# The values of the second cross-attention, made in the experts' stage instead of in layer 1's self-attention, and a block attention that ends in another order

## The chip, the core and the metric

The kernel runs on one core of one Trainium2 chip. The core has a matrix engine (TensorE, PE in the profile; its weight loads are listed as PEld), a vector engine (DVE), a scalar engine (ACT), GpSimd (POOL) and a sync engine (SP), which issues most of the DMAs. Matmuls write to eight banks of PSUM, called `bank[0]` to `bank[7]` here. The metric is the device time of one execution in microseconds; lower is better. Before the change it is 2019.05 us, the median of three runs (2017.79 to 2019.08).

## The reference, cut to what matters

Two decoder layers work on x of 8 sequences with 112 tokens of 512 features, in float32. Layer 0 has a self-attention, a cross-attention on a context of 8 x 375 rows, and a "block": an attention with 32 heads of 128 and a mixture of 32 experts of which each token takes 8, beside a shared expert. Layer 1 has a self-attention, a second cross-attention on the same context, and a feed-forward part.

```python
x = x + _L0_attn_ref(_layernorm(x), ...)
x = x + _L0_xattn_ref(_layernorm(x), ctx_2048, ...)
x = x + _L0_ffn_ref(_layernorm(x), ...)          # block attention, then experts
x = x + _L1_attn_ref(_layernorm(x), ...)
x = x + _L1_xattn_ref(_layernorm(x), ctx_2048, ...)
x = x + _L1_ffn_ref(_layernorm(x), ...)

# in _L0_ffn_ref, after the block attention
h = _rmsnorm(x, ln2_w)
router_scores = jax.nn.sigmoid(t @ Wr)
_, idx = jax.lax.top_k(router_scores + expert_bias[None, :], TOPK)

# in _L1_xattn_ref
k = (memory_tokens @ wk.T).reshape(B, M, NH, HD)
v = (memory_tokens @ wv.T).reshape(B, M, NH, HD)
```

The keys and values `k` and `v` of the second cross-attention depend on the context and on weights only, so they can be made at any time before they are used. The mask of the context leaves only its last 96 rows (`TAIL`) to be attended to here, so a sequence's values are one product of 96 x 512 by 512 x 512.

## The kernel before

The 896 tokens are kept as 7 tiles `x[t]` of 128 tokens. Each stage norms the tiles, turns them into `hT` (features on the partitions), projects, attends sequence by sequence, and adds the result to x or y.

**Who sets the order.** A planner orders the instructions of each engine ahead of time: among those that it takes to be ready, the one that comes first in the program goes first, and a tile gets a buffer when one comes free. Engines run their lists strictly in that order. Inside `with in_order():` the order of the program is kept on ACT, DVE, POOL and PE (not on SP). Such instructions all carry line L80 in the profile, since a helper issues them, and the profile leaves out the digits of names: `c1_wv` is `c_wv` there, `a1_wo` is `a_wo`.

**Weights and rows.** `load_w` loads 1 MB of weights into one of the six buffers of `wp`. Buffers are handed on as their last readers finish, and SP waits in its queue at a load whose buffer is not free. `normed_rows()` gives one of three buffers `xn`, which hold normed tiles, copies of products, and rows on their way to DRAM.

**The end of the block attention** (`l0_block_attention`). Head groups `hg` 0 to 7 go over the sequences `b` 0 to 7. Beside scores, softmax and averages, PE is given pieces of larger products from two lists by `fill`: `output_products(oT, wo, columns, p)` adds tiles 2p and 2p+1 of the attention's output to y, `last_output` adds tile 6 by way of bank 2. `wanted` holds how many pieces of each list a head group is to take, and the number given with `add` says how many averages must be done first. In the last group `prepare()` loads the constants of the experts (`expert_constants`), and the output products of the group itself follow, for p = 1 and 2 and the last tile after the loop. `gather_weights` copies the experts' weights into one DRAM table on SP, in 64 steps.

**The experts' norm and sort** (`l0_block_experts`). The phase `e0` opens when the attention's memory is free. `rmsnorm_rows_T` squares each tile on ACT (into bank 2 or 3, L1238), scales it on DVE (L1241), stores it to `hrows` for later gathers, and turns it on PE (L235) into `hT`. The router's matmuls (`lg`, L259) follow, then the sigmoid and, in program order, the sort: DVE finds the eight experts of each token and counts places, while PE runs the matmuls of the shared expert (`fill`, with `wgus`) between small counting matmuls. `names_of(t, n)` makes one-hot matrices on DVE, scales one on ACT, and adds them up on PE; `shared_out(t)` is the second matmul of the shared expert. Then POOL gathers the rows and weights of the 66 or more blocks, and the experts run. `tp_ps()` hands out banks 4 and 5 in turn for transposes.

**Layer 1's self-attention** (`l1_self_attention`) goes over 16 steps n, two for each sequence, and four more to empty the pipeline. In each step DVE adds biases to scores, finds minima, and sums exponentials; ACT takes the exponentials; POOL divides; PE makes scores, turns probabilities and averages. In steps 0 to 7 it has a projection to make besides (`chunk`). In steps 8 to 15 it makes the values of the second cross-attention instead (`far`), one sequence a step:

```python
                    if n >= B and n < 2 * B:
                        cT = work[0].tile([P, KC, TAIL], FP, tag="cTv", name="cTv")
                        nc.sync.dma_start(cT, a["ctxT"][n - B][:, :, EARLY:])
                        far = last_values(n - B, cT, c1_wv)
                        step(far)
                        step(far)
```

`last_values` multiplies on PE into a bank of `tp_ps()`, copies the 96 x 512 result into an `xn` buffer on ACT, and stores it to `far_values` in DRAM, from where the second cross-attention loads it. Each matmul call in float32 shows as two instructions in the trace.

Of the kernel before, what the change touches and what calls it, by code (L numbers as in the profile page):

```python
# [30 lines left out]
P = 128  # L31
# [6 lines left out]
KC = D // P  # L38
# [20 lines left out]
def decoder(ctx: ExitStack, tc: tile.TileContext, a, out: bass.AP):  # L59
# [874 lines left out]
    def l0_block_attention(y, hT, late, weights, prepare):  # L934
# [11 lines left out]
        with phase("f0", "tile") as p0:  # L946
# [215 lines left out]
            for hg in range(8):  # L1162
                wo = load_w(a["f0_wo"][hg], "f0_wo")
                oT = p0.tile([P, 4, NT], FP, tag="oT", name="oT", bufs=2)
                if hg < 7:
                    qT_next, wq = new_queries(hg + 1)
                else:
                    prepare()
                done = hg * B
                given[:] = 0, 0  # L1170
                wanted[:] = 16 * (hg < 7), 25 if hg else 9
                if rest:
                    add(1, output_products(*rest, 1), done - 3)
                if hg < 7:
                    for p in range(2):
                        add(0, query_products(qT_next, wq, p))
                else:
                    wanted[:] = 16, 13
                if rest:
                    if hg < 7:  # L1180
                        add(1, output_products(*rest, 2), done - 1)
                    else:
                        add(0, output_products(*rest, 2, 0), done - 1)
                    add(1, last_output(*rest[:2]), done)
                for b in range(B):
                    if b == 3 and hg in (2, 4):

                        kv = hg // 2 + 1
                        keys[kv % 2], values[kv % 2] = new_keys(), new_values()
                        nc.sync.dma_start(keys[kv % 2], far_k[kv - 2])  # L1190
                        nc.sync.dma_start(values[kv % 2], far_v[:, :, (kv - 2) * P : (kv - 1) * P])
                    scores(hg, qT, b)
                    fill((3 * b + 1) / (3 * B))
                    s, mn = find_minima()
                    waiting.append((hg, oT, b, s))
                    if undivided:
                        divide(*undivided.pop())
                    one = waiting.pop(0) if len(waiting) > 2 else None
                    if one:
                        pT = turned(one[3])  # L1200
                    fill((3 * b + 2) / (3 * B))
                    if one:
                        average(*one[:3], pT)
                        averaged[0] += 1
                        make_ready()
                    if b == 4:
                        columns = output_sums(wo)
                    if b == 5:
                        add(int(hg < 7), output_products(oT, wo, columns, 0, int(hg < 7)), done + 3)
                    undivided.append(exps(s, mn))  # L1210
                    gather_weights(hg * B + b, undivided[0][1])
                    fill((3 * b + 3) / (3 * B))
                while later:
                    rope_halves(*later.pop(0))
                qT, rest = qT_next, (oT, wo, columns)
            divide(*undivided.pop())
            for one in waiting:
# [2 lines left out]
                average(*one[:3], turned(one[3]))  # L1220
                averaged[0] += 1
                make_ready()
            add(1, output_products(*rest, 1))
            add(0, output_products(*rest, 2, 0))
            add(1, last_output(*rest[:2]))
            while lists[0] or lists[1]:
# [5 lines left out]
    def rmsnorm_rows_T(hT, rows, src, weight):  # L1232


        for t in range(NTT):
            sq = sc_ps()
            c = sm.tile([P, 2], FP, tag="rms", name="rms", bufs=8)
            A.activation(sq, src[t], AF.Square, scale=D**-0.5, accum_out=c[:, 0:1])  # L1238
            rsqrt(c[:, 1:2], c[:, 0:1], ONCE)
            xn = normed_rows()  # L1240
            V.tensor_scalar_mul(xn, src[t], c[:, 1:2])  # L1241
            nc.sync.dma_start(rows[t * P : (t + 1) * P, :D], xn)
            transpose_tile(hT, xn, t, weight)

    def expert_constants(pool, accs):

        wr = pool.tile([P, KC, NEXP], FP, tag="wr", name="wr")
        nc.sync.dma_start(wr, a["e0_wr"])
        ebias = pool.tile([P, NEXP], FP, tag="ebias", name="ebias")
        nc.sync.dma_start(ebias, a["e0_bias"].partition_broadcast(P))  # L1250
        wgus = wp.tile([P, 2, KC, NI], FP, tag="w", name="wgus")
        wds = wp.tile([P, 2, D], FP, tag="w", name="wds")
        nc.sync.dma_start(wgus[:, 0], a["e0_wsg"])
        nc.sync.dma_start(wgus[:, 1], a["e0_wsu"])
        nc.sync.dma_start(wds, a["e0_wsd"])
        zero = normed_rows()
        G.memset(zero, 0.0)
        for acc in accs:
            nc.sync.dma_start(acc[NT:, :], zero)
        return wr, ebias, wgus, wds  # L1260

    def l0_block_experts(yp, y, weights, accs, constants):

# [7 lines left out]
        with phase("e0") as p0:  # L1271
# [1 line left out]
            sort = ExitStack()  # L1273
            sp = sort.enter_context(tc.tile_pool(name="sort", bufs=1))
            hrows = tc.dram_tile([NT, D + NEXP], FP, name="hrows")
            wr, ebias, wgus, wds = constants


            def counted(name, rows, n, base, step, mult, dtype=FP, pool=None):
# [28 lines left out]
            for t in range(NTT):  # L1308
                V.tensor_scalar(token[:, t : t + 1], part, 128.0, 2.0**t, ALU.add, ALU.mult)
            hT = new_hT()  # L1310
            rmsnorm_rows_T(hT, hrows, y, ln2w)
            for t in range(NTT):
                G.tensor_tensor(y[t], y[t], x[t], ALU.add)
                nc.sync.dma_start(accs[0][t * P : (t + 1) * P, :], y[t])
# [62 lines left out]
            with in_order():  # L1377
# [123 lines left out]
                        T.matmul(names[:, :SLOTS], atlow[:, k, :], athigh[:, k, :],  # L1501
                                 start=(t == 0 and k == 0), stop=(t == NTT - 1 and k == TOPK - 1))

                shared_banks = bank[4:6] + bank[7:] + bank[2:4] + bank[:2]

                def shared_out(t):

# [8 lines left out]

                fill(4)
                product()
                names_of(0, 2)
                names_of(1, 3)  # L1520
                names_of(2, 3)
                product()
# [1 line left out]
                product()  # L1524
                token_weights()
                for t in range(4, NTT):
                    shared_out(t - 4)
                    names_of(t, 0)

                name = sp.tile([P, SLOTS], FP, tag="name", name="name")  # L1530
                V.tensor_copy(name, names[:, :SLOTS])
# [125 lines left out]
    def l1_self_attention():  # L1657
# [2 lines left out]

        wq, wk_, wv, wo, c1_wv = (
            load_w(a[n], n) for n in ("a1_wq", "a1_wk", "a1_wv", "a1_wo", "c1_wv")
        )
        with phase("a1", "tile") as p0:


# [190 lines left out]

            next_hT = [None]  # L1860
            with in_order():
                chunk = out = vals = far = None
                norms = [next_rows(t) for t in range(NTT)]
                take_scores(0)
                mask_queries(1)
                for n in range(STEPS + 4):


                    b, odd = divmod(n - 4, 2)
                    sums = average(b) if 0 <= b < B and not odd else None  # L1870
                    if n < STEPS:
                        add_biases(n)
                        if not odd:
                            vals = values(n // 2)
                        step(vals)
                    elif n == STEPS:
                        next_hT[0] = new_hT()
                    exps(n - 1, 0)
                    exps(n - 1, 1)
                    if odd and n < STEPS:  # L1880
                        step(vals)
                    turn_probs(n - 2, 0)
                    turn_probs(n - 2, 1)
                    for _ in range(3):
                        step(chunk)
                    step(out)
                    if n + 2 < STEPS:
                        mask_queries(n + 2)
                    done = [t for t in range(NTT) if b * S < (t + 1) * P <= (b + 1) * S]
                    out = project_out(done[0]) if done and odd and b >= 0 else None  # L1890
                    step(out)
                    step(sums)
                    if n + 1 < STEPS:
                        take_scores(n + 1)
                    exps(n - 1, 2)
                    exps(n - 1, 3)
                    step(sums)
                    turn_probs(n - 2, 2)
                    chunk = project(*chunks[n + 1], 1, one_mm_ps) if n < 7 else None
                    step(chunk)  # L1900
                    if n >= B and n < 2 * B:
                        cT = work[0].tile([P, KC, TAIL], FP, tag="cTv", name="cTv")
                        nc.sync.dma_start(cT, a["ctxT"][n - B][:, :, EARLY:])
                        far = last_values(n - B, cT, c1_wv)
                        step(far)
                        step(far)
                    turn_probs(n - 2, 3)
                    step(chunk)
                    if n < STEPS:
                        find_minima(n)  # L1910
                    divide(n - 1)

                    for at, tiles in ((17, (0, 1, 2)), (18, (3, 4)), (19, (5,))):
                        for i in range(3):
                            for t in tiles:
                                if n == at + (i > 1):
                                    step(norms[t])
# [431 lines left out]
```

## Time and profile before

| | |
|---|---|
| median of three runs | 2019.05 us (2017.79 to 2019.08) |
| the profiled execution | 2019.05 us, span 2017.3 us |
| mean granted clock of PE | 0.97 |
| busy: PE, DVE, POOL, ACT | 1903.8, 969.2, 911.1, 687.3 us |
| chain that ended last | PE 61%, DVE 12%, POOL 9% of the span |

| stage | from to, us |
|---|---|
| layer 0's self-attention and cross-attention | 0 to 415 |
| block attention, end of its last PE work | 870.9 |
| norm and router, to the sigmoid | 870.9 to 898.7 |
| sort, to the first gather of rows | 898.7 to 941.3 |
| experts | 941.3 to 1340 |
| layer 1's self-attention, its steps | 1420 to 1605 |
| second cross-attention, feed-forward | to 2017.3 |

A row of the profile names the engine, the line, the operation, what it writes and reads (out<-in) and how often. A time in brackets with an arrow is idle time of the engine just before, and what ended it. Engines work side by side; a shorter row shortens the run only where it lies on the chain that ends last. The clock is the share of full speed that the chip granted to PE in a stretch of time.

### The profile page before, as it was taken

To read this page: it belongs to the slowest core of one execution; us is meant where nothing else is said; L and a number is where in the kernel's file an instruction comes from. 1 tells how busy PE (TensorE), PEld (TensorE's weight loads), DVE (VectorE), ACT (ScalarE), POOL (GpSimd) and SP (SyncE) were. 2 spreads that over 40 slices of the span, in tenths; PEclk is the share of its full clock that TensorE was granted. 3 is DMA by queue.
4 is the path that set the end of the run, shared out by engine and by line. 5 is a ranking of instruction groups with operands and counts; after the bars stand their busy time and mean duration, and the time that the engine had idled before them with its cause. 6 is when DMAs were issued, how large, how long until landed. Compare 5 with 4: busy or idle time off the path is not lost.

```text
span 2017.3 us, 28226 instructions
## 1 busy us (share of the span) xinstructions
PE 1903.8 (94%) x10345; PEld 1240.5 (61%) x10345; DVE 969.2 (48%) x1993; ACT 687.3 (34%) x1939; POOL 911.1 (45%) x1099
## 2 busy tenths in 40 slices
PE   8999999999999999988999999998899898799999
PEld 4545654456666666765788888864555554455568
DVE  4562466486676676445222222224787556622260
ACT  3543321044444444522111111122566535432200
POOL 2253042256767765632566666622454212334371
PEclk9999988999999999969999999999999899999999
DMA  4105010234444445536977776652001120211100
GB/s 179 43 22 164 24 58 28 74 136 143 158 131 160 146 136 171 193 132 233 255 200 173 169 190 156 157 142 68 22 24 38 48 68 15 85 42 42 42 6 31
DMA packets 87470, 217.05 MB, mean 108 GB/s; under 512 B 33427, under 2 KB 41363, under 8 KB 78228
## 3 DMA queue, kind: packets, MB, share of 16 engines
q1 hardware_dynamic: 63028, 141.61, 21.0%
q0 software_dynamic: 24288, 73.47, 14.7%
q8 instruction: 87, 1.43, 0.3%
q14 instruction: 67, 0.55, 0.1%
HBM read 248.98 MB, written 82.43 MB: 164 GB/s over the span
## 4 chain that ended last, share of the span: by engine, by line
PE 61%; DVE 12%; POOL 9%; issue 8%; ACT 4%; DMA 4%; SPq 1%; POOLq 0%; ACTq 0%; DVEq 0%
PE bank L843 22%; PE bank L80 18%; PE bank L259 13%; POOL acc L80 4%; POOL hrow L80 2%; PE bank L1072 2%; DMA acc<-ob,row_out 2%; PE bank L1107 2%; DVE qs L928 2%; PE bank L1063 1%; POOL st L80 1%; DVE mxs L80 1%; PE bank L1100 1%; DMA hrow<-hrows,row_in 1%; PE bank L235 1%
## 5 line engine op out<-in xcount | busy, mean ns | idle before, releaser
L80 PEld LDWEIGHTS bank<-hbT,wb 128*128 128x128 f32 x1408 | 164.1, 192 | 20.4 <-issue 20.4
L80 DVE TENSOR_TENSOR hidb<-sgb,bank 128x256 f32<-128x256 f32 x66 | 27.8, 421 | 289.5 <-ACT sgb L80 228.2
L80 PE MATMUL bank<-hbT,wb 128*128 128x128 f32 x1408 | 164.3, 275 | 0.0
L80 POOL TENSOR_TENSOR st<-st,rec 112x448 f32<-112x448 f32 (+1 forms) x95 | 82.9, 904 | 147.7 <-DVE rec L80 77.6
L1089 ACT ACTIVATE s<-s,mn 112x112 f32<-112x112 f32 x256 | 97.5, 382 | 130.2 <-DVE mn L1083 120.7
L932 POOL TENSOR_TENSOR qT<-qT,qs 128x448 f32<-128x448 f32 x64 | 78.2, 1222 | 107.4 <-DVE qs L928 107.4
L80 POOL DMA_INDIRECT acc<-ob,row_out x66 | 106.3, 1611 | 35.0 <-issue 18.3
L80 ACT ACTIVATE st<-st,mxs 112x112 f32<-112x112 f32 (+1 forms) x383 | 111.0, 379 | 0.0
L80 ACT ACTIVATE sgb<-bank 128x256 f32<-128x256 f32 x66 | 25.4, 384 | 202.6 <-PE bank L80 173.1
L80 POOL DMA_INDIRECT wb<-weights,wrow x44 | 46.4, 1055 | 94.1 <-PE bank L80 71.1
L1096 POOL TENSOR_TENSOR s<-s,rec 112x448 f32<-112x448 f32 x64 | 64.7, 1013 | 52.3 <-DVE rec L1095 46.9
L80 POOL DMA_INDIRECT hrow<-hrows,row_in x66 | 63.9, 968 | 48.2 <-DVE free L80 24.1
L80 ACT ACTIVATE ob<-bank,pw 128x512 f32<-128x512 f32 x66 | 45.3, 687 | 116.4 <-PE bank L80 116.4
L80 PE MATMUL bank<-wb,hidb 128*128 128x512 f32 x176 | 84.2, 602 | 0.0
L843 PE MATMUL bank<-tok,sums 128*128 128x448 f32 x192 | 78.1, 541 | 1.9 <-DVE tok L827 1.4
L843 PE MATMUL bank<-osum,osums 128*128 128x256 f32 x288 | 74.6, 383 | 1.9 <-POOL osums L820 1.6
L1072 PEld LDWEIGHTS bank<-kT,qT 128*112 128x112 f32 x512 | 61.8, 178 | 21.7 <-DVE s L1078 9.2
L1072 PE MATMUL bank<-kT,qT 128*112 128x112 f32 x512 | 63.3, 263 | 6.2 <-DVE s L1078 6.2
L928 DVE TENSOR_TENSOR qs<-xn,shape_consts 64x448 f32<-64x448 f32 x84 | 67.4, 802 | 1.5
L843 PEld LDWEIGHTS bank<-osum,osums 128*128 128x128 f32 x288 | 52.5, 190 | 24.2 <-issue 14.7
L80 PE MATMUL bank<-ident,st 112*112 112x112 f32 (+1 forms) x384 | 51.8, 269 | 15.1 <-POOL st L80 11.3
L1047 POOL TENSOR_TENSOR y<-y,oc 128x256 f32<-128x256 f32 x63 | 50.8, 811 | 32.4 <-DVE y L1045 29.8
(447 smaller groups left out, 4373.7 us busy)
## 6 DMA issues: line engine op xcount, KB each, us to landing
weights<-in_e_wg SPq DMA_DIRECT2D x64, 256.0 KB
weights<-in_e_wu SPq DMA_DIRECT2D x64, 256.0 KB
weights<-in_e_wd SPq DMA_DIRECT2D x64, 256.0 KB
f_wq<-in_f_wq SPq DMA_DIRECT2D x8, 1024.0 KB
f_wo<-in_f_wo SPq DMA_DIRECT2D x8, 1024.0 KB
cTe<-in_ctxT SPq DMA_DIRECT2D x8, 558.0 KB
f_wg<-in_f_wg SPq DMA_DIRECT2D x4, 1024.0 KB
f_wu<-in_f_wu SPq DMA_DIRECT2D x4, 1024.0 KB
```

The costliest lines, as they stand in the source:

```text
L80: done = issue(*args, **kw)
L235: T.transpose(tp[:, c * P : (c + 1) * P], src[:, c * P : (c + 1) * P], ident)
L259: T.matmul(dst, lhs(k), rhs(k), start=(k == 0), stop=(k == n - 1))
L843: T.matmul(dst, lhs(k), rhs(k), start=first and k == 0, stop=k == terms - 1, skip_group_check=True)
L928: V.tensor_tensor(qs[lo : lo + 64], src[hi : hi + 64], sin0[lo : lo + 64].unsqueeze(1).to_broadcast([64, HB, S]), ALU.mult,)
L932: G.tensor_tensor(d, d, qs, ALU.add)
L1047: G.tensor_tensor(d, d, more, ALU.add)
L1063: T.matmul(pp, oT[:, k, t * P : (t + 1) * P], wo[:, k, :], start=(k == 0), stop=(k == KC - 1))
L1072: T.matmul(bank[5][:S, j * S : (j + 1) * S], qT[:, j, tok], keys[hg // 2 % 2][:, tok], start=True, stop=True)
L1089: A.activation(s[:, j, :], s[:, j, :], AF.Exp, bias=mn[:, j : j + 1], scale=-1.0, accum_out=den[:, j : j + 1])
L1096: G.tensor_tensor(s, s, rec.unsqueeze(2).to_broadcast([S, 4, S]), ALU.mult)
L1107: T.matmul(po[:, : 4 * S], values[hg // 2 % 2][:, b, :], pT.rearrange("p j q -> p (j q)"), start=True, stop=True)
```

## The change

The eight products leave layer 1's self-attention. The weight `c1_wv` is loaded in `expert_constants`, so it holds one of the six weight buffers from the last head group on. Sequences 0 to 4 are made between the normed tiles (`rmsnorm_rows_T` becomes a generator that pauses after each tile), sequences 5 to 7 in the sort: before the first `names_of`, and beside `shared_out` of t = 4 and 5. Their context is loaded into `wbuf[3]`, a buffer for expert weights that is not yet in use.

The squares of the norm go to bank 7 instead of banks 2 and 3. The output of the shared expert uses the banks in the order 7, 2, 3, 0, 1, 4, 5 instead of 4, 5, 7, 2, 3, 0, 1. In the last head group of the block attention the second list is given a share of 16 pieces instead of 13, and the output product of tiles 2 and 3 is added to it in the last sequence of the loop instead of after the loop.

```diff
@@ l0_block_attention
                 else:
-                    wanted[:] = 16, 13
+                    wanted[:] = 16, 16
...
                     if b == 4:
                         columns = output_sums(wo)
+                    if b == 7 and hg == 7:
+                        add(1, output_products(oT, wo, columns, 1), done + 5)
...
-            add(1, output_products(*rest, 1))
             add(0, output_products(*rest, 2, 0))
             add(1, last_output(*rest[:2]))
@@ rmsnorm_rows_T
-            sq = sc_ps()
+            sq = bank[7]
...
             transpose_tile(hT, xn, t, weight)
+            yield
@@ expert_constants
         nc.sync.dma_start(wds, a["e0_wsd"])
+        c1_wv = load_w(a["c1_wv"], "c1_wv")
         zero = normed_rows()
...
-        return wr, ebias, wgus, wds
+        return wr, ebias, wgus, wds, c1_wv
@@ l0_block_experts
+            def values_of_next(b):
+                cT = wbuf[3].rearrange("p m (b n) -> p (m b n)", b=1).rearrange(
+                    "p (b k n) -> p b k n", b=B, k=KC)[:, b]
+                nc.sync.dma_start(cT, a["ctxT"][b][:, :, EARLY:])
+                return last_values(b, cT, c1_wv)
...
-            rmsnorm_rows_T(hT, hrows, y, ln2w)
+            for t, _ in enumerate(rmsnorm_rows_T(hT, hrows, y, ln2w)):
+                if t < 5:
+                    all_of(values_of_next(t))
...
-                shared_banks = bank[4:6] + bank[7:] + bank[2:4] + bank[:2]
+                shared_banks = bank[7:] + bank[2:4] + bank[:2] + bank[4:6]
...
                 fill(4)
                 product()
+                far = [values_of_next(b) for b in range(5, B)]
+                next(far[0])
                 names_of(0, 2)
+                all_of(far[0])
...
                 for t in range(4, NTT):
+                    if t < 6:
+                        next(far[t - 3])
                     shared_out(t - 4)
                     names_of(t, 0)
+                    if t < 6:
+                        all_of(far[t - 3])
@@ l1_self_attention
-        wq, wk_, wv, wo, c1_wv = (
-            load_w(a[n], n) for n in ("a1_wq", "a1_wk", "a1_wv", "a1_wo", "c1_wv")
-        )
+        wq, wk_, wv, wo = (load_w(a[n], n) for n in ("a1_wq", "a1_wk", "a1_wv", "a1_wo"))
...
-                    if n >= B and n < 2 * B:
-                        cT = work[0].tile([P, KC, TAIL], FP, tag="cTv", name="cTv")
-                        nc.sync.dma_start(cT, a["ctxT"][n - B][:, :, EARLY:])
-                        far = last_values(n - B, cT, c1_wv)
-                        step(far)
-                        step(far)
```

## The prediction

> **What bounds the kernel now.** I read the page first (PE is busy for 94% of the span), then the busy times by stage, because one average says little here, and then the two places that the change touches: the end of the block attention with the norm and sort behind it, and the self-attention of layer 1. The columns are the window, its length, busy time of PE, weight loads, DVE, ACT and POOL, the granted clock and the DMA share. The rows are the norm, the sort, and layer 1's steps without and with the moved products.
> ```profile
> 870.90:898.70 27.80, 21.64 (x89) 18.77 (x90) 12.21 (x29) 8.48 (x23) 11.09 (x19) 0.54 0.51 185
> 898.70:941.30 42.60, 37.56 (x139) 18.37 (x140) 28.41 (x89) 11.40 (x16) 3.98 (x3) 0.90 0.40 152
> 1420.00:1504.20 84.20, 72.45 (x652) 46.68 (x654) 67.96 (x141) 54.68 (x172) 41.90 (x42) 0.98 0.08 26
> 1504.20:1590.00 85.80, 80.80 (x752) 49.53 (x743) 58.76 (x130) 58.80 (x188) 37.96 (x39) 1.00 0.14 36
> ```
> While the values are made, PE is busy for 80.8 of 85.8 us at full clock. In the norm it is busy too, but at a clock of 0.54. The rows of the moved tile give the price, and the chain of waits shows who ends last:
> ```profile
> L80 PE MATMUL bank<-c_wv,cTv x64: 591/592/670, 1507.1 to 1586.1; 128*96 128x512 f32 x64
> ...
> 1525.93 18.05 PE bank L80 x180
> 1543.98 0.02 issue
> 1544.00 0.58 ACT xn L80
> 1544.59 0.43 ACT pT L80
> 1545.02 0.12 ACT sink L80
> 1545.13 2.23 ACT st L80 x8
> 1547.36 0.43 ACT pT L80
> ```
> One pair of steps takes 21.9 us: 18.05 us of PE without a gap, then 3.8 us of ACT that begins with the copy (xn) of the moved product. DVE waits. Its own list (start, duration, and in brackets the idle time and its releaser) shows a step without the product, and then the stalls once it is there:
> ```profile
> 1496.01 2.18 DVE L80 TENSOR_REDUCE mxs<-st 112x4 f32<-112x448 f32 x4
> ...
> 1503.06 0.62 DVE L80 SCALAR_TENSOR_TENSOR st<-bank,dist 112x448 f32<-112x448 f32 x1 [0.30 <-PE bank L80]
> 1503.60 0.68 DVE L80 TENSOR_TENSOR x<-x,bank 128x512 f32<-128x512 f32 x1
> 1504.20 2.19 DVE L80 TENSOR_REDUCE mxs<-st 112x4 f32<-112x448 f32 x4
> ...
> 1522.56 0.63 DVE L80 SCALAR_TENSOR_TENSOR st<-bank,dist 112x448 f32<-112x448 f32 x1 [2.40 <-PE bank L80]
> 1524.68 0.62 DVE L80 SCALAR_TENSOR_TENSOR st<-bank,dist 112x448 f32<-112x448 f32 x1 [1.49 <-PE bank L80]
> ```
> At the end of the block attention the first squares wait for the last tile, and PE then waits for them:
> ```profile
> 871.60 0.60 ACT L1238 ACTIVATE bank<-y 128x512 f32<-128x512 f32 x1 [7.24 <-DVE y L1066]
> ...
> 875.32 1.12 PE L235 MATMUL bank<-ident,xn 128*128 128x128 f32 x4 [4.47 <-DVE xn L1241]
> ```
>
> **The change part by part.** The sum is made against the profiled execution, 2019.05 us (span 2017.3 and 1.75 around it), which is also the median of the runs.
>
> *Removed from layer 1.* Eight products of 8 matmul rows. In the PE list one product holds PE for 3.45 us (1540.37 to the next row's weights, at 0.43 us a row), so 27.6 us leave PE; 8 ACT copies of 0.58 us leave ACT, 16 DMA issues leave SP. PE no longer ends last: a pair without them needs 21.9 - 2 x 3.45 - 1.0 idle = 14 us of PE and 14.9 - 1.2 = 13.7 us of ACT, but 15.1 us of DVE (by a window of one pair). So DVE sets the pace. The one interval that already runs so, from the minima of step 7 (1496.01) to those of step 8 (1504.20), takes 8.19 us with the 0.68 us addition to x, which comes in every second step; half of it off, 7.9 us a step. From step 8 to step 15 (1504.20 to 1579.64) a step takes 75.44 / 7 = 10.78 us, so 7 x 2.9 = 20.1 us go. The eighth product lies in the tail (1583.05 to 1586.5, with ACT's copy behind it): 3.6 us more. Together -23.7. Bounds: -27.6, if all of PE's time goes; and -10.9, if a step stays at the 9.74 us between steps 8 and 9, the shortest with a product in it (7 x 1.04 + 3.6). I take -23.7, as the 7.9 us step is an observed one.
>
> *Added to the norm.* Five products, 17.3 us of PE at full clock, five ACT copies, five loads. What PE must do here otherwise: 56 router matmuls, 4.96 us for 24 at half clock, so an estimated 0.103 us each at full, 5.8; 28 transposes at 0.11 us (8 in 0.93 us at full clock in layer 1), 3.1. With the products 26.2 us, from 870.9 to 897.1; with 1.5 us for waits on copies and loads, 898.6, where the sigmoid starts at 898.72 today. The stage is free only because it is now run at half clock; the cover is the clock. Two things speak for full clock. The squares go to bank 7 instead of banks 2 and 3, so they no longer wait for the last output product to be read out of bank 2 (7.24 us above), and output tiles 2 and 3 are asked for a batch earlier; so early tiles can be normed and turned before 870.9 and their router products can fill the 4.47 us gap. And a dense stream brings the clock back: the shared experts' matmuls start at 898.5 and the clock is 1.0 from 903.7. If the gap stays, the first 5.2 us are at half clock, +2.6; a load that comes late adds more: 558 KB of context took 4.1 us from issue to its reader (177.35 to 181.46), a 192 KB piece at most that, +4.1; and DVE, copies and the three xn buffers (now for 12 tiles instead of 7) may add 2. Where all tiles are early, -5 (the gap). I take 0, range -5 to +9.
>
> [...]
>
> *Added to the sort.* Three products, 10.4 us of PE. PE idles 2.05 us before the first names (917.39) and 2.98 us before the fifth (933.65), and four output matmuls behind that gap take 3.39 us instead of 1.95, being at half clock: 6.5 us of cover, so +3.9. If none of it is in the right place +10.4; if DVE and ACT set the pace (DVE is busy 28 of 42.6 us) less. Most of it is next to a product in program order, so +3.9, range +2 to +8. ACT's one-hot scalings queue behind the copies; 3 x 0.58 us lie in ACT's idle time (6.5 us before one).
>
> *Start of the experts.* The shared output of tiles 5 and 6 now sits in banks 4 and 5, where the first two row transposes go; the last of its copies ends at 947.66 today, the first transposes start at 946.83. +0.5 (0 to +1).
>
> *End of the block attention.* PE work is the same and PE is full from 820 to 870.9 (0.2 us idle); order alone gives 0. The weight of the values now takes a weight buffer from head group 7 on. Its load waits for the query products (PE reads that buffer until 801); behind it on SP are copies of expert weights, last issued at 867 and first gathered at 912.7, so 40 us of cover. DVE's column sums then wait for a buffer that is read until 832; behind them on DVE are score minima, and the first product that needs them is at 841.9 today. The next load (cross-attention keys' weight) waits on SP until 845 instead of 834. 0, range -1 to +3. SP's loads of context come behind the wait for the whole attention pool (870.9); behind them are row stores that are ready at 875.
>
> Sum: -23.7 + 0 + 3.9 + 0.5 + 0 = -19.3, so 1999.8 us.
>
> **The rivals.**
> *PE stays at half clock through the norm* (ends slower). Each product then takes 6.9 us, 34.5 together, and the small work 18; from 875 the sigmoid comes at 928, 29 us later than now. Sum -23.7 + 29 + 4.4 = +9.7, 2029. It decides from 19.3 us on, so if two thirds of the stage (19.3 / 29) are at half clock. For it: the clock was 0.5 from 873 to 903 although PE was busy from 879, with transposes and matmuls of 32 columns; the new products are split by just those. Against it: one 6.9 us product is longer than the 5.2 us that the dense stream needed. [...] Chance 0.07.
>
> *Another wait takes the product's place in layer 1*: POOL's division or ACT's exponentials, at 9.74 us a step. -10.9 + 4.4 = -6.5, 2012.5. For it: in steps 2 to 6, with projections in place of products, a step took 11.08 us and DVE stood 2.1 us of it. Against: those waits are for the projection's own banks. Chance 0.13.
>
> *The products get no cover in norm and sort*: loads late, the order of PE fixed ahead wrongly, +9 and +8. -23.7 + 17.5 = -6.2, 2012.8. Chance 0.13.
>
> That the products stay where they are is not possible: the calls in layer 1 are gone. Forecast: 0.67, between 1991 and 2008.
>
> **How the numbers follow.** The time is the forecast's. The range goes from -29 (full gain of PE's time, early norm, small costs) to the two middle rivals, 2013; outside are the first rival and a small rest. A measurement of this kernel tells 0.2%, 4 us, from no change. Faster: the forecast, and most of the middle rivals, 0.67 + 0.23 = 0.90; within 0.2%: 0.03; slower 0.07.
>
> **What would show it.** In the profile after: minima of layer 1's steps 8 to 15 7.9 us apart, PE idle there, DVE without waits of 1.49 and 2.40 us; squares of the first tiles before the last output product; the clock near 1.0 from 880 on; the sigmoid at 899 within 5 us and the first row gather near 946 (941.34 now). The prediction is wrong if steps stay above 9.5 us or if the sigmoid comes after 908.

## The result, and the profile after

The changed kernel takes 2009.51 us (median of seven runs, 2007.35 to 2012.19), the kernel before 2017.79 us in the same session (2012.81 to 2026.84). The ratio is 0.9962, 95% interval 0.9945 to 0.9980: 8 us faster, where 19 were forecast. The profiled execution took 2007.35 us with a span of 2005.6, so the two spans differ by 11.7 us.

| landmark in the trace, us | before | after | difference |
|---|---|---|---|
| last four instructions of the last output product of the block attention, start (PE) | 868.96 | 870.62 | +1.7 |
| sigmoid | 898.72 | 912.94 | +14.2 |
| first gather of rows | 941.34 | 956.03 | +14.7 |
| first expert's matmul | 948.78 | 966.23 | +17.5 |
| last expert's matmul | 1334.64 | 1345.87 | +11.2 |
| minima of layer 1's step 8 | 1504.20 | 1515.46 | +11.3 |
| minima of step 15 | 1579.64 | 1572.71 | -6.9 |
| start of the second cross-attention (c_wq) | 1617.40 | 1609.07 | -8.3 |
| end | 2017.3 | 2005.6 | -11.7 |

Layer 1 gave back 18.2 us in seven steps. Before that, 17.5 us had been lost by the first expert's matmul, 12.6 of them between the end of the block attention and the sigmoid; the experts' stage gave 6.2 us back, and 11 us of loss were left. Each figure is of one profiled execution: two profiles of one kernel (early_loads and early_again below) lie 3.3 us apart at the first landmark, so a difference of that size there need not come from the change. The windows of the changed kernel are the norm, the sort, and layer 1's steps without and with the (now removed) products. Columns as before.

```profile
872.50:912.90 40.40, 33.91 (x133) 18.95 (x132) 8.68 (x24) 6.59 (x15) 9.80 (x18) 0.87 0.66 212
912.90:956.00 43.10, 41.98 (x160) 19.91 (x160) 28.33 (x89) 12.88 (x19) 3.97 (x3) 1.00 0.49 173
1431.30:1515.50 84.20, 75.13 (x653) 48.28 (x655) 67.59 (x141) 54.58 (x172) 41.86 (x42) 0.94 0.04 14
1515.50:1574.00 58.50, 50.84 (x667) 36.45 (x656) 53.13 (x119) 49.95 (x163) 34.20 (x35) 1.00 0.08 29
```

The norm has the five products in it and a clock of 0.87, and yet takes 12.6 us more than before. The sort takes 0.5 us more with three products in it. PE's list in the norm shows where the time lies:

```profile
870.62 1.88 PE L1063 MATMUL bank<-f_wo,oT 128*128 128x512 f32 x4
872.34 0.60 PE L235 MATMUL bank<-ident,xn 128*128 128x128 f32 x4
875.21 1.86 PE L259 MATMUL bank<-wr,hT 128*128 128x32 f32 x8 [2.28 <-DVE hT L241]
879.50 6.64 PE L259 MATMUL bank<-c_wv,wb 128*96 128x512 f32 x8 [2.42 <-DMA wb<-in_ctxT]
```

One tile is normed and turned early, as hoped. Then PE waits 2.28 us for its copy, runs the first router tile at half clock (1.86 us; the later ones take 0.97), and waits 2.42 us for the first context. The first product, also at half clock, takes 6.64 us; the later ones take 3.6. SP's list says why the context came late:

```profile
871.07 0.38 SPq L157 DMA_DIRECT2D a_wq<-in_a_wq  x1
871.55 0.52 SPq L1120 DMA_DIRECT2D weights<-in_e_wg  x1
...
873.45 7.20 SPq L1286 DMA_DIRECT2D wb<-in_ctxT  x8
```

Layer 1's first weight (1 MB) stands on SP behind two stores, which wait for DVE until 867.8 and for POOL until 870.6. Behind it come three copies of expert weights (256 KB each), and only then the eight context loads, which take SP 7.2 us to issue. The first context is at its reader 6.0 us after its issue (873.45 to 879.50). Before the change that weight was out of the way much earlier:

```profile
847.21 0.36 SPq L157 DMA_DIRECT2D a_wq<-in_a_wq  x1
```

The values' weight now holds one of the six buffers from the last head group on, and the loads behind it move back: the keys' weight from 834.12 to 844.99, and layer 1's first weight from 847.21 to 871.07. The new order alone does not do that (844.92 in order_only, below).

In layer 1 the chain of waits has become this (one pair of steps):

```profile
1532.07 5.47 PE bank L80 x112
1537.54 0.72 issue
1538.26 0.94 POOL st L80
...
1539.25 5.57 PE bank L80 x48
...
1545.92 2.22 ACT st L80 x8
```

The next pair begins at 1548.61, so a pair takes 16.5 us for 21.9 before. PE's long run of 18.05 us is now two runs of 5.5, with POOL's division between them. DVE still waits a little for PE, 0.30 and 1.06 us where it was 2.40 and 1.49:

```profile
1522.52 0.63 DVE L80 SCALAR_TENSOR_TENSOR st<-bank,dist 112x448 f32<-112x448 f32 x1 [0.30 <-PE bank L80]
1523.06 2.19 DVE L80 TENSOR_REDUCE mxs<-st 112x4 f32<-112x448 f32 x4
...
1530.87 0.62 DVE L80 SCALAR_TENSOR_TENSOR st<-bank,dist 112x448 f32<-112x448 f32 x1 [1.06 <-PE bank L80]
```

### The profile page after: what moved, and what is told of

Read it like the earlier page. It is cut to its first block, busy times and chain, and to the rows that moved or that the text cites. A ratio compares the mean times of both kernels' runs of the same rounds, so it can differ in the third digit from the quotient of the medians.

```text
span 2005.6 us, 28210 instructions
## 1 busy us (share of the span) xinstructions
PE 1893.5 (94%) x10345; PEld 1233.2 (61%) x10345; DVE 965.0 (48%) x1993; ACT 689.6 (34%) x1941; POOL 907.9 (45%) x1099
## 5 line engine op out<-in xcount | busy, mean ns | idle before, releaser
L80 PEld LDWEIGHTS bank<-hbT,wb 128*128 128x128 f32 x1408 | 164.5, 192 | 20.5 <-issue 20.1
```

The costliest lines, as they stand in the source:

```text
L80: done = issue(*args, **kw)
```

## The experiments

Three theories stood against each other. Theory 1: the removal was sized rightly, and the time was lost where the products went. Theory 2: the removal itself was worth less. Theory 3: the new order at the attention's end cost the time. The first four kernels separate them; the others then ask what in the norm it was. All were timed beside the kernel before. In the table, "norm" is the time from the start of the last four instructions of the last output product to the sigmoid, and "experts" the time from the first to the last expert's matmul, both from the profile.

| kernel | median us | ratio to before, 95% | norm | experts |
|---|---|---|---|---|
| before | 2018 | 1 | 29.8 | 385.9 |
| changed | 2009.5 | 0.9962 (0.9945 to 0.9980) | 42.3 | 379.6 |
| l1_only | 1993.8 | 0.9883 (0.9859 to 0.9908) | 29.4 | 385.6 |
| order_only | 2016.8 | 0.9988 (0.9977 to 0.9998) | 24.8 | 387.7 |
| no_products | 1989.6 | 0.9858 (0.9843 to 0.9872) | 24.4 | 384.5 |
| three_in_sort | 2003.2 | 0.9931 (0.9915 to 0.9947) | 24.7 | 382.8 |
| early_loads | 1995.1 | 0.9889 (0.9875 to 0.9904) | 31.5 | 381.3 |
| early_again | 1998.0 | 0.9914 (0.9900 to 0.9929) | 31.2 | 379.8 |
| first_early | 1998.2 | 0.9904 (0.9888 to 0.9921) | 31.2 | 383.0 |
| wq_later | 2009.0 | 0.9961 (0.9945 to 0.9976) | 38.6 | 380.7 |
| early_own | 2001.6 | 0.9927 (0.9909 to 0.9945) | 30.1 | 380.9 |
| banks | 2008.9 | 0.9959 (0.9946 to 0.9973) | 42.3 | 382.7 |
| early_banks | 2001.1 | 0.9924 (0.9907 to 0.9941) | 31.3 | 386.2 |
| four_moved | 1996.9 | 0.9904 (0.9890 to 0.9918) | 22.1 | 380.0 |
| five_moved | 2002.2 | 0.9928 (0.9911 to 0.9946) | 23.7 | 386.4 |

**Removal, order, products.** In the first kernel the products are taken from layer 1 and made nowhere:

```diff
@@ before: l1_self_attention
-                    if n >= B and n < 2 * B:
-                        ...
-                        step(far)
-                        step(far)
@@ expert_constants
+        for b in range(B):
+            nc.sync.dma_start(far_values[:, b, :], zero[:TAIL])
```

> The kernel before, with the eight products left out of layer 1 and made nowhere: the second cross-attention's values are read as zeros, stored once from the zeroed tile of the experts' constants. It measures the removal alone. Theory 1 (the removal was sized right, the time is lost where the products went): the seven steps take 57 us for the 75.4 of before, and from the minima of step 8 to the last feed-forward 23 us go, as the changed kernel's trace shows, so 23 us under the kernel before, ratio 0.9885. Theory 2 (the removal itself is worth only what the whole change gave): 8 to 12 us under it, 0.995.

The ratio 0.9883 is 23.6 us of 2018; by the interval it is 18.6 to 28.5. From step 8 to step 15 the minima go from 1503.70 to 1560.93, 8.18 us a step. Theory 2 falls.

The second has only the new order (wanted 16 and 16, the third group's products added at the last step, squares in bank 7); the products stay in layer 1.

> The kernel before, with only the new order at the end of the block attention (third group's products added at the last step, 16 wanted, squares in bank 7); the products stay in layer 1. Theory 1: nearly nothing, 0 to 3 us slower (the last output product ended 1.65 us later in the changed kernel), the sigmoid at 896 to 902. Theory 3 (the new order is what cost the time: a clock that falls again, a later end): 8 us or more slower, the sigmoid after 906.

Theory 3 falls as well: the order alone wins 2.4 us by the ratio (0.4 to 4.6 by the interval), where Theory 1 had it level or up to 3 us slower. Its norm shrinks from 29.8 to 24.8 us, and the last output product ends only 0.3 us later (its last four instructions start at 869.27 for 868.96). What the norm is without products, in the new order, this kernel's window shows:

```profile
871.00:894.00 23.00, 19.02 (x98) 15.50 (x97) 7.84 (x23) 4.12 (x10) 9.10 (x18) 0.78 0.54 187
```

PE is idle for 4 us there, and the clock is 0.78. That is the cover which the products could use.

The third is the changed kernel without products in the norm and the sort:

```diff
@@ after: l0_block_experts
             for t, _ in enumerate(rmsnorm_rows_T(hT, hrows, y, ln2w)):
-                if t < 5:
-                    all_of(values_of_next(t))
+                pass
...
-                far = [values_of_next(b) for b in range(5, B)]
...
```

> The changed kernel with the eight products made nowhere (their matmuls, copies, context loads, weights and stores are left out, and the values are read as zeros). The changed kernel less this one is what the products cost in the norm, the sort and the start of the experts. Theory 1: 13 to 17 us, so this kernel is 21 to 25 us under the kernel before, with the sigmoid at 896 to 902 and the first expert's matmul near 950. Theory 3 (the order): within 3 us of the changed kernel, 8 to 12 us under the kernel before.

0.9962 - 0.9858 = 0.0104, so the products cost 21 us in their new places by the runs (17.4 by the two profiled spans), more than the 13 to 17 that Theory 1 expected.

The fourth splits them: products 0 to 4 back in layer 1, 5 to 7 in the sort.

> The changed kernel, but products 0 to 4 are made in layer 1's steps 8 to 12 as before, and only the last three in the sort. Theory 1 with a sort that covers its three: three eighths of 23 us is won in layer 1 and 0 to 3 us are lost in the sort and the order, so 5 to 9 us under the kernel before, and the sigmoid at 896 to 902. If the sort's three cost their 10.4 us of PE in full, it is 2 us over the kernel before.

It gained 14 us, beyond what was expected: with three of eight moved it beats the full change by 6 us. Its sort takes 43.1 us for 39.9 without products, so the sort's three cost 3.2 us for 10.4 us of PE. The loss lies with the five in the norm.

**When the contexts come.** The next kernel loads the contexts of products 0 to 4 into a weight buffer in the attention's last steps:

```diff
@@ l0_block_attention
+                    if b == 6 and hg == 7:
+                        c1 = wp.tile([P, 5, KC, TAIL], FP, tag="w", name="c1ctx")
+                        for i in range(5):
+                            nc.sync.dma_start(c1[:, i], a["ctxT"][i][:, :, EARLY:])
+                        next_contexts.append(c1)
@@ values_of_next
+                if b < 5:
+                    return last_values(b, next_contexts[0][:, b], c1_wv)
```

> The changed kernel, with the contexts of products 0 to 4 loaded during the last steps of the block attention into a weight buffer, not after it into the experts' buffer; nothing else. Theory A (the norm's products would have found the predicted cover, had their loads not been late): the waits of 2.28 and 2.42 us and the half clock of the first product (3.0 us) and first router tile (0.9 us) go, so the sigmoid comes at 903 to 906 and the whole is 7 to 9 us under the changed kernel, ratio to the kernel before 0.992. Theory B (PE had no free time in the norm, each product costs its 3.6 us wherever its data lie): at most 3 us under the changed kernel, sigmoid after 909.

It was run twice, because near relatives of it gained less:

> The kernel of the early loads once more. The profiles put its gain over the changed kernel at 6.6 us (spans 1999.0 and 2005.6), its runs at 14.5 us, and two kernels with the same loads and another bank order or other buffers at 7 us. If 7 us is right: 0.992 to 0.993 of the kernel before. If 14.5 is right: 0.988 to 0.990.

The two give 0.9889 and 0.9914, which is 10 to 15 us under the changed kernel; the profiles' norms are 10.8 and 11.1 us shorter. Theory A holds, with a larger size than expected. The same kernel gave ratios that are 5 us apart, though, so a difference of that size between two kernels of this study is not certain.

The edit also does more than it was meant to. The early contexts take a weight buffer, and with that layer 1's first weight moves on SP from 871.07 to 889.96 in the second run (893.20 in the first), and the three copies of expert weights are issued before 863. So the 1.75 MB ahead of the contexts are gone as well; the kernel wq_later, below, has that part alone. PE's list and the window of the second run:

```profile
871.09 2.74 PE L259 MATMUL bank<-c_wv,c1ctx 128*96 128x512 f32 x6
873.66 0.97 PE L259 MATMUL bank<-wr,hT 128*128 128x32 f32 x8
...
874.94 3.60 PE L259 MATMUL bank<-c_wv,c1ctx 128*96 128x512 f32 x8
```

```profile
870.60:900.10 29.50, 28.79 (x132) 16.92 (x131) 9.83 (x24) 6.82 (x15) 9.74 (x18) 1.00 0.72 240
```

The first product now follows the first transposes without a gap, so PE never falls to half clock (1.00 for the whole norm) and is idle for 0.7 us. Term by term, out of 11.1 us: idle time 6.49 against 0.71 us, 5.8; the first product 6.64 against 2.74 us, 3.9 (of it 0.86 are two instructions that moved into the attention); the first router tile 1.86 against 0.97 us, 0.9. Together 10.6.

Is it each context, or the first?

```diff
+                        c1 = wp.tile([P, 1, KC, TAIL], FP, tag="w", name="c1ctx")
+                        for i in range(1):
...
+                if b == 0:
+                    return last_values(b, next_contexts[0][:, b], c1_wv)
```

> The changed kernel with only product 0's context loaded early; those of products 1 to 4 are loaded after the block attention as in the change. If the loss sits at the front (the first wait and the half clock behind it), this one load brings most of what the five early loads brought: from the last output product to the sigmoid 31 to 34 us for the 42.3 of the change, and the whole at 0.990 to 0.9935 of the kernel before. If each late context costs its own wait: 36 us or more, and 0.995.

The first alone brings all of it: a norm of 31.2 us and 0.9904. While product 0 runs, the next context arrives: product 1 follows at 877.05, and PE waits for none of the contexts. Here too layer 1's first weight has moved back (to 892.10). Whether one early context would be enough with the 1.75 MB still ahead of the others was not tried.

And is it the 1 MB weight ahead of them on SP, or the buffer that is only free with the attention's end?

```diff
+        for i in range(2):
+            spare_w = wp.tile([P, 4, 512], FP, tag="w", name="spare_w")
+            nc.sync.dma_start(spare_w[:, 0, :28], a["cols"])
         with phase("e0") as p0:
```

> The changed kernel, with two small dummy loads that turn the ring of weight buffers on by two, so that layer 1's first weight load (1 MB) is no longer ahead of the contexts on SP; the contexts still go into the experts' buffer after the block attention. Theory A1 (that load, held until the attention's end, made the contexts late): the first product starts 3 to 5 us earlier, with no half clock, the sigmoid at 904 to 909, and 5 to 9 us under the changed kernel. Theory A2 (the buffer, free only with the attention's end, made them late): sigmoid after 911 and within 2 us of the changed kernel.

Some of both, and no time in the end. The 1.75 MB are gone from the front, SP issues the first context when the last output product ends (874.40), and the context is there 3.5 us later at most (877.87), where it took 6.0. The first product starts 5.5 us after the last four instructions of the output product, not 8.9, and the norm is 3.7 us shorter; but the wait of 2.28 us and the half clock remain (5.35 us for the first product). First_early, which has the early first context besides, has a norm that is 7.3 us shorter still. So of some 11 us, 3.7 came with the 1.75 MB and 7.3 with the first context. The sigmoid, at 910.95, fits neither theory; the whole time is what Theory A2 had. The sort then takes 45.9 us for 43.1, because this row meets a longer wait (1.09 us in the changed kernel) and the clock falls again:

```profile
916.60 0.18 PE L80 MATMUL bank<-ones,earlier 128*32 128x1 bf16 x1 [2.60 <-DVE earlier L80]
```

```profile
911.00:920.00 9.00, 6.40 (x18) 2.75 (x18) 6.46 (x41) 2.13 (x3) 0.00 (x0) 0.79 0.22 86
```

**Buffers and banks.** In early_own the copies of products 0 to 4 go to a free part of `wbuf[2]`, not to the three `xn` buffers:

> The kernel of the early loads, with the copies of products 0 to 4 in a free part of an experts' weight buffer in place of the three row buffers that the norm uses. If the shared row buffers hold the norm back (DVE waited 2.0, 4.5 and 0.7 us for them in the changed kernel, PE 1.56 and 0.23 us for DVE and ACT), 1 to 3 us under the early loads alone. If PE is the bound, DVE's waits are hidden and it is within 1 us of it.

No gain in the whole (0.9927). The norm is 1.1 to 1.4 us shorter, as the first branch of the expectation had it, so the shared row buffers do hold it back a little. But the last output product comes 3 to 6 us later than in the two runs of the early loads (874.84). Why is not known; those two runs are 3.3 us apart there themselves.

In the kernel banks only the order of the shared output's banks is changed:

```diff
-                shared_banks = bank[7:] + bank[2:4] + bank[:2] + bank[4:6]
+                shared_banks = bank[7:] + bank[2:3] + bank[4:6] + bank[3:4] + bank[:2]
```

> The changed kernel, with the shared output in the order of banks 7, 2, 4, 5, 3, 0, 1, so that banks 4 and 5, where the first experts' rows are turned, are copied third and fourth and not last. If this order is what the start of the experts lost (PE idle for 2.58 us before the first rows, ACT waiting 4.65 and 2.11 us for stores between the copies): first expert's matmul 8 us after the first row gather in place of 10.2, and 1.5 to 3 us under the changed kernel. If the experts' stage makes up for its start anyway (it ran 6 us shorter in the changed kernel): within 1 us of it.

The first expert starts 7.0 us after the first gather and not 10.2, and the end is the same (0.9959). The experts' stage makes up for its start. The waits of PE in it, in the kernel before, the changed one and this one (total, times, longest), say how:

```profile
PE bank L80 <- DMA hrow<-hrows,row_in: 6.0, 7, 2.6
```

```profile
PE bank L80 <- DMA hrow<-hrows,row_in: 1.0, 2, 0.7
```

```profile
PE bank L80 <- DMA hrow<-hrows,row_in: 4.8, 4, 3.2
```

An expert that starts earlier waits for its gathered rows. All fifteen traces fit this: where the first expert starts 7.0 to 7.9 us after the first gather, PE waits 3.7 to 8.5 us for rows in the stage, and where it starts 8.4 to 10.9 us after it, 0.4 to 3.4. Both changes together give the same picture:

> All eight products moved, contexts of 0 to 4 loaded early, and the shared output in the bank order 7, 2, 4, 5, 3, 0, 1. If the experts' stage makes up for its start, it is the early loads' 0.989 again, and a second measure of it; if PE's wait of 2.6 us before the first experts' rows counts here, 2 to 3 us less.

The experts take 386.2 us in it for 379.8 to 381.3 with the early loads alone, with 7.0 us of waits for rows. At 0.9924 the kernel is level with the early loads alone (0.9889 and 0.9914) or slower; the 2 to 3 us less did not come.

**Fewer products in the norm.** The last two kernels move four and five products: 5 to 7 in the sort, 0 (and 1) in the norm with early contexts, the others in layer 1. They differ in one thing more: with four moved, the copy of product 0 has a buffer of its own; with five, the copies use the shared row buffers.

> The changed kernel with only four products moved: 5 to 7 in the sort, and product 0 at the start of the norm, its context loaded early and its copy in a buffer of its own; products 1 to 4 stay in layer 1's steps 9 to 12. If the wait for the first tiles of the norm (3.98 us in the kernel without products, with the clock at half for 13 us behind it) is cover that a product can use: product 0 is free and the clock stays up, so 3 to 7 us under the kernel with three in the sort, at 1996 to 2000. If it is not, product 0 costs 3.5 us there and saves 3.0 in layer 1: level with it at 2003.

> As the kernel with four products moved, but products 0 and 1 at the start of the norm with early contexts, and copies in the shared row buffers; 2 to 4 stay in layer 1. With product 0 alone the norm still has a wait of 1.84 us and a clock at half for some 10 us behind it (4.7 us lost). If the second product takes the place of these, it is free and 3 us are saved in layer 1: 1992 to 1995. If it costs its 3.5 us of PE, level with four moved at 1997.

Product 0 is free: the norm takes 22.1 us with it, 24.7 without, and the kernel is 5 us under three_in_sort. Product 1 adds 1.6 us to the norm for its 3.6 and saves 3.5 in the seven steps of layer 1, but the kernel is 5 us slower than with four. In its profile the experts' stage takes 6.4 us more: PE waits 7.1 us for rows in it (1.5 in four_moved), and the clock falls to 0.91 (960 to 980) after one wait of 2.95. So the forecast for it missed, by a wait that this study did not set out to steer.

All eight moved with one early context (0.9904) and four moved (0.9904) both beat the kernel before and the change; between these the intervals show no difference.

## Why the prediction had the sign and not the size

In the profiled spans 11.7 us came of the 19.3 that were forecast. Against the sum, 12.6 us more were spent in the norm, 4.1 less came from layer 1, 1.7 more went at the end of the block attention and 2.3 at the start of the experts; the sort cost 3.4 us less, and the experts' stage and the second cross-attention, which were not in the sum, were 6.2 and 3.4 us shorter.

*Removed from layer 1*, -23.7: right for the removal alone, which measures 23.6 us. That the two lie so close is in part luck: the interval is 10 us wide, and the seven steps gave 18.2 us for 20.1. In the changed kernel the profile shows 18.2 + 1.4 = 19.6. The terms differ a little: a step takes 8.18 us, not 7.9, because PE waits for POOL's division and ACT's exponentials once more in each pair, so that DVE does not quite set the pace; the tail gives 4.8 us in l1_only, not 3.6, and 1.4 in the changed kernel (why less is not known; in order_only, with the products in place, the tail is 1.8 us shorter than in the kernel before). The second rival named these very waits; it priced them at 9.74 us a step, and they cost 0.3.

*Added to the norm*, 0 (-5 to +9): this is the step that failed, and in it the terms "a load that comes late" (+4.1) and the half clock behind a gap (+2.6), which were left to the range. With the first context in time the norm takes 31.2 us for 29.8 before: the zero was near for a norm whose loads are there. Late, it takes 42.3, and that is +12.6. PE waited 4.7 us for the first tile's copy and the first context (2.28 and 2.42), and the half clock cost 3.9 us (3.0 in the first product, 0.9 in the first router tile). Two things were wrong. The price of the load was taken from a row with no large load just ahead of it on SP; here 1 MB and 0.75 MB were ahead, and 4.1 us became 6.0. The prediction followed what the values' weight does to the next load on SP (the keys' weight, at 845, as it came), but not to the one behind it, which so came to stand ahead of the contexts. And the terms were summed as if each were possible alone, but they follow from each other: without the first context there is a gap (4.70 us in the two waits), behind its first part the clock is at half (0.50 from 875.30 to 885.54), and at half clock the first product takes 6.64 us where the later ones take 3.6. The cover (PE's idle time and half clock) lay at the front of the norm, at just the place where no context could be yet. That loads wait for the end of the attention was in the prediction, under "behind them are row stores"; that the first product stands behind them too was not drawn from it. The sum of PE's work, 26.2 us, also left out the shared expert's matmuls that run in the norm, 3.9 us in the changed kernel. The rival "no cover in norm and sort" had the mechanism (loads late), at +9 for the 12.6; its sort's share did not come, and that its 2012.8 us lies nearer to the result than the forecast is partly luck: what neither sum had nearly cancels (9.6 us less in the experts' stage and the second cross-attention, 8.1 us worse in layer 1, the attention's end and the experts' start).

*Added to the sort*, +3.9: measured 0.5 against before, and 3.2 against the new order without products. The 6.5 us of cover were there (10.4 - 3.2 = 7.2), and the sort is shorter in the new order already (39.9 us in no_products, 40.8 in order_only, for 42.6).

*Start of the experts*, +0.5: 2.8 in the trace, and worth nothing, as the kernel banks shows, since the stage gives it back in waits for rows (6.2 us shorter here). That the experts' stage makes up for some of a late start was not in the sum at all.

*End of the block attention*, 0 (-1 to +3): +1.7 in the trace, inside the range, but not by what the prediction looked at, the weight buffers. What came is a square that now runs early on ACT and waits there for its tile, ahead of a copy that PE needs:

```profile
850.59 0.60 ACT L1239 ACTIVATE bank<-y 128x512 f32<-128x512 f32 x1 [4.35 <-POOL y L1047]
...
851.22 0.51 ACT L1102 COPY pT<-bank 112x448 f32<-112x448 f32 x1
851.75 1.28 ACT L191 ACT_TABLE_LOAD   x1
```

```profile
851.78 1.86 PE L1107 MATMUL bank<-pT,v 112*128 112x448 f32 x2 [2.77 <-ACT pT L1102]
```

Before, PE had no such gap. The trace of order_only is the same up to this wait (2.77 us, until 851.77). There the clock stays at 1.00 behind it, and the last output product ends 0.3 us later than before; in the changed kernel the clock falls to half behind it, and the end comes 1.35 us later than that. So of the +1.7 most is the half clock, and little the wait itself. The order still pays, for its norm is 5.0 us shorter.

The rival of a half clock through the whole norm was wrong: it lasts to 885 and is gone with the first product. Of the signs that were to show it, the steps and DVE's waits came as told, the squares ran early, but the sigmoid at 912.94 was past the 908 that was named as the point of failure. Open remains why the second cross-attention (from c_wq to the first matmul on tok) takes 138.7 us here and 142.1 before, 3.4 of the 11.7 us: the kernels of this study scatter between 138.7 and 142.9, in no order that fits one of the edits.

## What to carry to other kernels

Work that is moved into idle time needs its data at the beginning of that idle time. Follow the moved step's first load through its queue and its buffer's release, and if it can't land before the gap opens, the gap is no cover (here 42.3 us of norm with the late load, 31.2 with the early one). Follow the other loads too, for a tile that takes a buffer earlier can move a large load to just ahead of it (here 1 MB from 847.21 to 871.07). Here one early load for the first step was enough, with nothing large ahead of the loads of the rest. Where a gap, a half clock and a late load stand at the same place, price them as one chain and not as separate ends of a range. And ask of the stage behind whether it waits for something else anyway: a start that is lost or won before such a wait need not reach the end (in the kernel banks 3.2 us won at the start of the experts left the time at 0.9959, for 0.9962).

## What the runs showed of the hardware

The granted clock fell behind gaps of PE of 2.77 us (the changed kernel), 2.60 (wq_later) and 1.84 (four_moved), and did not fall behind the 2.77 us of order_only. The traces give the times of its changes. In the profiles of the kernel before and of the changed kernel it changes 40 times each, between 1.00 and 0.50, and in both all changes lie a whole number of times 3.41 us apart (in the changed kernel at 851.40, 854.82, 875.30 and 885.54, among others). The rows below are stretches of that length. Of the 2.77 us gap above, 2.4 lie in the stretch just before the fall at 851.40 in the changed kernel (first row); of the same gap in order_only, 1.8 lie in the stretch of the second row:

```profile
847.99:851.40 3.41, 1.02 (x6) 0.57 (x4) 1.04 (x2) 0.81 (x3) 2.49 (x4) 1.00 0.98 383
849.94:853.35 3.41, 1.58 (x6) 1.12 (x7) 0.00 (x0) 2.74 (x6) 0.61 (x1) 1.00 1.01 378
```

Behind 1.02 us of work in its stretch the changed kernel is at half clock until 854.82, and the two instructions of 448 columns behind the gap take 1.86 us. With 1.58 us in its stretch order_only keeps 1.00 (from 836 to 871), and they take 1.02. Twelve profiles with the new order have this gap in PE's list (2.77 to 2.79 us). In ten of them the two instructions behind it take 1.61 to 1.86 us; in early_own they take 1.02, and the four behind them 1.79 where 1.03 is usual; only in order_only does nothing behind it run slower. Two executions of one kernel differ: behind the gap the half clock lasts 6.8 us in early_loads and 3.4 in early_again. The gap of 2.60 us in wq_later is of the same kind: the clock falls at 916.29, after a stretch with 1.13 us of work. That it is the work in the stretch before that decides is the author's estimate from these rows; a limit does not follow from them.

Busy time alone does not tell the clock in these rows. The first row below is four_moved: 1.82 us of transposes and router matmuls, more than the 1.58 above, and the clock falls at its end (876.88). The other two are the kernel before, with PE busy throughout, on transposes and 24 router instructions in a row (5.2 us): the clock stays at 0.50.

```profile
873.47:876.88 3.41, 1.82 (x17) 1.83 (x18) 2.83 (x14) 1.90 (x3) 2.34 (x9) 1.00 0.37 142
879.73:883.14 3.41, 3.41 (x19) 3.41 (x17) 1.83 (x8) 0.43 (x1) 1.73 (x3) 0.50 0.55 207
883.14:886.55 3.41, 3.41 (x18) 3.41 (x18) 0.24 (x1) 0.00 (x0) 1.19 (x1) 0.50 0.44 156
```

Why it stays there is not shown.
